# Two chained cross-attentions: stores of weighted values and loads of x moved on the DMA queue of the first half

## The chip, the cores and the metric

The kernel runs on one core of a Trainium2 chip. The core has a matrix engine (TensorE, PE in the profile), a vector engine (VectorE, DVE), a scalar engine (ScalarE, ACT), a general engine (GpSimd, POOL) and SyncE (SP), which here does nothing but issue DMAs. Every engine works through its own list of instructions in order and waits on semaphores for the others. The metric is the device time of one execution in microseconds (us). A profiled execution gives the trace from which single durations are read.

## The reference

Two cross-attention layers over the same 128 context tokens for each of two batches, 2048 tokens of 512 features each, all in float32:

```python
# layer 0: 16 heads of 64
qh = (x @ Wq + bq);  kh = (ctx @ Wk + bk);  vh = (ctx @ Wv + bv)
attn = einsum('bqhd,bkhd->hbqk', qh, kh) * mask
attn = exp(attn - max(attn)) * mask           # one maximum over everything
attn = attn / (sum(attn, -1) + 1e-15)
x = layernorm(einsum('hbqk,bkhd->bqhd', attn, vh) @ Wo + bo + x) * gamma + beta
# layer 1: 16 heads of 32, ordinary softmax, no mask
x = layernorm(softmax(q @ k.T / sqrt(32)) @ v @ Wo.T + bo + x) * gamma1 + beta1
```

The maximum of layer 0 is over all heads, batches and tokens, so no block of it can be finished before all scores of layer 0 exist.

## The kernel before

The 4096 tokens are cut into 8 tiles of 512 (`t`), taken in 4 pairs (`p`); the 16 heads into 4 groups of 4 (`g`). A *block* is one tile and one group: four heads, 128 keys, 512 tokens each.

The *first half* of the program computes layer 0 up to the weighted values. It is a loop of 16 steps `i` (`p = i // 4`, `g = i % 4`); each step takes both tiles of a pair for one group, so two blocks, called A (tile 2p) and B (tile 2p+1) below. The order is written out by hand, each engine keeps it, and DMAs stand in SyncE's list where the program names them. A step runs:

- loads for later: in pairs 1 and 2 (steps 4 to 11) the x of the next pair, in 512 KB halves, one in the steps with g = 0 and g = 2, two in those with g = 1 (`load_x`, L236, issued by SyncE); masks by POOL's queue (L242).
- `queries_pair` (L355 on TensorE, 28 matmuls in seven products): the queries of both blocks, put together from shared products by additions on VectorE (L367, L369). Between them, `exponentials0` of the two blocks of the step before: VectorE takes the maxima that were loaded back (L438, L439), ScalarE exponentiates (L442), POOL multiplies by the mask (L443). A's comes behind the first product, B's near the end.
- `sums_of_folded` in some steps (L478): denominators of the step before the last, copied out of the accumulators by VectorE and ScalarE (L449) and stored (L450).
- `scores0` of A: eight matmuls (L404), then VectorE masks the scores and takes a maximum for each key and pair of heads (L417, tile `top`). The maxima have to be the same on all 128 partitions, so they go through DRAM: a store of 1 KB (L426, `top_dram`) and a load of all 256 numbers to every partition, 128 KB (L429, tile `every`). The load waits, on SyncE, until the store has landed.
- `attend0` of A of the step before: TensorE multiplies probabilities and values (L499; L492 for denominators where they aren't folded), ScalarE copies the result out (L503), SyncE stores it, 512 KB (L504, `u_dram`).
- `scores0` of B, then `attend0` of B of the step before, in the same way.

The last step's maxima (both blocks) stay on the chip (`last4`) and are neither stored nor loaded. `shift` (L464) and `fold` (L470) prepare the folded denominators. Tile `u` has three buffers, x has four buffers in each of two pools, which the pairs use in turn. `wkv1`, the weights of keys and values of layer 1 (2 MB), is loaded at step 4, L542 and L543, and the output weights of layer 0 (2 MB) at step 13, L515.

The *second half* then normalises the weighted values, projects them, and runs layer 1; its order is written out too, and it is not touched.

Of the kernel before, what the change touches and what calls it, by code (L numbers as in the profile page):

```python
# [24 lines left out]
def two_cross_attentions(  # L25
# [28 lines left out]
    nc = tc.nc  # L54
# [14 lines left out]
    def where(t):  # L69
        return t // SPB, (t % SPB) * TB  # L70
# [18 lines left out]
    def sc_tiles(name, shape):  # L89
        return [p_sc.tile([P, *shape], F32, tag=f"sc{n}", name=f"{name}_{n}") for n in range(2)]  # L90
# [4 lines left out]
    def av_tile(name):  # L95
        return p_av.tile([P, TB], F32, tag="av", name=name)
# [28 lines left out]
    def chunks(w):  # L125
        return w.rearrange("(c p) m -> p c m", p=P)
# [6 lines left out]
    def row(pool, v, name, tag=None):  # L133
# [5 lines left out]
    u_dram = {  # L139
        (t, g): dram.tile([P, 2 * TB], F32, tag=f"u_{t}_{g}", name=f"u_{t}_{g}")  # L140
        for t in range(NB)
        for g in range(NG)
    }
    top_dram = {
        (t, g): dram.tile([P, 2], F32, tag=f"top_{t}_{g}", name=f"top_{t}_{g}")
        for t in range(NB)
        for g in range(NG)
    }
# [67 lines left out]
    with tc.tile_pool(name="w1", bufs=1) as w1, tc.tile_pool(name="a2", bufs=2) as a2, tc.tile_pool(  # L216
# [13 lines left out]
        def load_x(t, halves=range(2)):  # L230

            b, q0 = where(t)
            pool, tag = (big, "big") if t // 2 % 2 else (xs, "xt")
            for h in halves:
                xt = pool.tile([P, 2, TB], F32, tag=tag, name=f"xt_{t}_{h}")
                nc.sync.dma_start(xt, xT[b, q0 // TB, h])  # L236
                xts.setdefault(t, []).append(xt)

        def load_mask(t):
            b, q0 = where(t)  # L240
            m = a4.tile([P, TB], F32, tag="mask", name=f"mask_{t}")
            nc.gpsimd.dma_start(m, maskT[b, :, q0 : q0 + TB])  # L242
            return m
# [145 lines left out]
            add(c12, product(3, s4[:, g], b22, mm_tile), c12)  # L389

        tops0, probs0, pairs0 = {}, {}, {}
        FOLDED = [n for n in range(NB // 2 * NG - 2) if n % NG != NG - 2]
        last4 = w1.tile([P, 4], F32, tag="last4", name="last4")
        order = [(2 * p + n, g) for p in range(NB // 2) for g in range(NG) for n in range(2)]

        def scores0(t, g):

            b, _ = where(t)
            st = sc_tiles(f"st_{t}_{g}", [2, TB])
            for n in range(2):  # L400
                q = queries.pop((t, 2 * g + n))
                for j in range(2):
                    rows = slice(j * DK, (j + 1) * DK)
                    nc.tensor.matmul(  # L404
                        st[n][:, j, :], k0[rows, 2 * g + n, b * K : (b + 1) * K], q[rows, :],
                        start=True, stop=True,
                    )
            pair = fours.tile([P, 2, 2, TB], F32, tag="p1", name=f"sm_{t}_{g}")
            n0 = 2 * (order.index((t, g)) - len(order) + 2)
            if n0 >= 0:  # L410
                top = last4[:, n0 : n0 + 2]
            else:
                top = a2.tile([P, 2], F32, tag="top", name=f"top_{t}_{g}")
            pairs0[t, g] = pair
            for n in range(2):
                sm = pair[:, n]
                nc.vector.tensor_tensor_reduce(  # L417
                    out=sm, in0=st[n], in1=masks[t].unsqueeze(1).to_broadcast([P, 2, TB]),
                    scale=1.0, scalar=-3.4028234e38, op0=ALU.mult, op1=ALU.max,
                    accum_out=top[:, n : n + 1],  # L420
                )
                probs0[t, 2 * g + n] = sm
            if n0 >= 0:
                return

            nc.sync.dma_start(top_dram[t, g], top)  # L426
            every = a2.tile([P, 2 * P], F32, tag="every", name=f"every_{t}_{g}")
            flat = top_dram[t, g].rearrange("p n -> (p n)").unsqueeze(0)
            nc.sync.dma_start(every, flat.to_broadcast([P, 2 * P]))  # L429
            tops0[t, g] = every  # L430
# [16 lines left out]
        def store_sums(t, g, ps, copy=nc.scalar.copy):  # L447
            den = a2.tile([P, TB], F32, tag="den", name=f"dens0_{t}_{g}")
            copy(den, ps)  # L449
            nc.sync.dma_start(  # L450
                den_rows(den_dram, t, g), den.rearrange("(j n) q -> j n q", n=32)[:, 0, :]
            )
# [32 lines left out]
        def attend0(t, g):  # L485

            b, _ = where(t)
            p = [probs0[t, 2 * g + j // 2][:, j % 2, :] for j in range(4)]
            if order.index((t, g)) // 2 not in FOLDED:
                ps = av_tile(f"den0_{t}_{g}")  # L490
                for j in range(4):
                    nc.tensor.matmul(ps[32 * j : 32 * (j + 1), :], ones, p[j], start=True, stop=True)  # L492
                store_sums(t, g, ps)
            u = a3.tile([P, 2, TB], F32, tag="u", name=f"u0_{t}_{g}")
            for half in range(2):
                ps = av_tile(f"psu0_{t}_{g}_{half}")
                for j in range(4):
                    d = (4 * g + j) * DK + half * 32
                    nc.tensor.matmul(  # L499
                        ps[32 * j : 32 * (j + 1), :], v0[:, b, d : d + 32], p[j],  # L500
                        start=True, stop=True,
                    )
                nc.scalar.copy(u[:, half, :], ps)  # L503
            nc.sync.dma_start(u_dram[t, g], u.rearrange("p j q -> p (j q)"))  # L504

        bo0s, g0s = row(const, bo0, "bo0"), row(const, g0, "g0")
        b0cs = columns(const, b0c, "b0c")
# [12 lines left out]
        for i in range(len(order) // 2):  # L520
            p, g = i // NG, i % NG
            steps0 = order[2 * i : 2 * i + 2]
            if p == 0 and g == 2:
                for t in (2, 3):
                    load_x(t)
                    masks[t] = load_mask(t)
            elif 0 < p < NB // 2 - 1:
                for n in ((0,), (1, 2), (3,), ())[g]:
                    load_x(2 * p + 2 + n // 2, (n % 2,))
                if g > 1:  # L530
                    t = 2 * p + g
                    masks[t] = load_mask(t)
            if p == 0:
                for e in (2 * g, 2 * g + 1):
                    keys0(e)
            if i == 1:
                for n in range(E // TB):
                    values0(1, n)
            if i == 4:
                w = w1.tile([P, 2 * ND, TB], F32, tag="first", name="wkv1")  # L540
                wk1s, wv1s = w[:, :ND, :], w[:, ND:, :]
                nc.sync.dma_start(wk1s, chunks(wk1))  # L542
                nc.sync.dma_start(wv1s, chunks(wv1))  # L543
            if i == 12:
                sums0(0, w1, "sums0", 1)
            if i == 13:
                load_wo0()

            if i == 0:
                queries0(0, 0)  # L550
                queries0(0, 1)
            else:
                queries_pair(p, g, order[2 * i - 2 : 2 * i])
                if i - 2 in FOLDED:
                    sums_of_folded(i - 2)
            if i == len(order) // 2 - 1:
                for n in range(NG):
                    fetch_u(0, n)
            scores0(*steps0[0])
            if i == 0:  # L560
                queries0(1, 0)
                queries0(1, 1)
                weight_sums(1)
            else:
                if i - 1 in FOLDED:
                    shift(i - 1, 0)
                    fold(i - 1, 0)
                attend0(*order[2 * i - 2])
                if i - 1 in FOLDED:
                    shift(i - 1, 1)  # L570
            if i == 0:
                token_sums_1(0)
            elif g == NG - 1 and p + 1 < NB // 2:
                token_sums_1(p + 1)
            scores0(*steps0[1])
            if i == 0:
                for n in range(E // TB):
                    values0(0, n)
                token_sums_2(0)
                weight_sums(2)  # L580
            elif i < len(order) // 2 - 1:
                attend0(*order[2 * i - 1])
                if i - 1 in FOLDED:
                    fold(i - 1, 1)
            if g == NG - 1 and p + 1 < NB // 2:
                token_sums_2(p + 1)
            if i in (1, 2):
                weight_sums((3, 0)[i - 1])
# [45 lines left out]
        for n in range(2):  # L634
            t, g = order[n - 2]
# [439 lines left out]
    def store(t, i):  # L1075
        b, q0 = where(t)
        nc.sync.dma_start(out[b, q0 + i * P : q0 + (i + 1) * P, :], ys.pop((t, i))[0])
# [91 lines left out]
    t = NB - 1  # L1169
# [78 lines left out]
```

## Time and profile before

| | us |
|---|---|
| time before, median of 3 runs | 953.12 |
| lowest, highest | 951.63, 958.23 |
| profiled execution | 951.15 |
| its span, first to last instruction | 949.4 |

One profiled execution was read, with a mean granted TensorE clock of 0.995 of full speed. Of the DMA queues, SyncE's (q1) moved 155.64 MB in 65536 packets, with 49.2% of the time of the 16 DMA engines. Of the span's 30-us stretches between 40 and 370 us, TensorE is busy all 30 us in four, and for at least 28.2 us in every one. The first half's steps lie between some 30 and 370 us.

How to read it: times of instructions are from the start of the span. A timeline line has start, duration, engine, source line, operation, output and input tiles, count, and in brackets the idle time of that engine before it and what ended it. In a list of waits a line has who waited for whom, then the total in us, how often, and the longest. SPq is SyncE's issuing side: a line there is the issue of a DMA, not its transfer. Matmuls are pipelined and their ends are modelled, so a distance between starts says more of TensorE than its busy share.

### The profile page before, as it was taken

How to read it: one execution, taken by the hardware profiler on the slowest of the kernel's cores; microseconds unless marked ns; L12 is line 12 of the kernel's file. 1: busy time of each engine (PE TensorE's matmuls, PEld its weight loads, DVE VectorE, ACT ScalarE, POOL GpSimd, SP SyncE). 2: the span in 40 equal slices, each digit the busy share in tenths (PEclk: the TensorE clock that was granted, in tenths of full speed). 3: DMA queues.
4: the chain of work that ended last, by engine and by line, in shares of the span. 5: the costliest groups of instructions: out<-in, count | busy, mean ns of one | idle time of the engine just before them, and what ended most of it. 6: DMA issues, size and time to landing. Idle time of an engine off the chain costs nothing.

```text
span 949.4 us, 12453 instructions
## 1 busy us (share of the span) xinstructions
PE 924.2 (97%) x4404; PEld 444.0 (47%) x4404; DVE 695.3 (73%) x1026; ACT 378.2 (40%) x837; POOL 491.3 (52%) x403
## 2 busy tenths in 40 slices
PE   8999999999999999999999999999999999999996
PEld 4444333333333334356474564654744645546532
DVE  1577777877887885044929959969779699599777
ACT  1055445445645554213535333325234153154051
POOL 1043335534543335864682683764854936735343
PEclk9999999999999999999999999999999999999998
DMA  9414253323322525662987757656758567444401
GB/s 337 139 51 144 58 167 112 117 79 96 95 68 63 153 76 206 179 193 67 305 278 234 298 165 261 250 183 235 253 167 295 165 229 305 137 161 155 133 35 56
DMA packets 67326, 159.07 MB, mean 168 GB/s; under 512 B 10496, under 2 KB 14336, under 8 KB 63680
## 3 DMA queue, kind: packets, MB, share of 16 engines
q1 hardware_dynamic: 65536, 155.64, 49.2%
q0 software_dynamic: 1152, 2.10, 0.8%
q8 instruction: 35, 0.57, 0.3%
q10 hardware_dynamic: 576, 0.53, 0.2%
q14 instruction: 27, 0.22, 0.1%
HBM read 101.46 MB, written 56.78 MB: 167 GB/s over the span
## 4 chain that ended last, share of the span: by engine, by line
PE 45%; DVE 12%; DMA 2%; issue 2%; POOL 2%; ACT 1%; SPq 0%; POOLq 0%; DVEq 0%; ACTq 0%
PE pso L690 17%; PE pso L1039 8%; PE psq L829 6%; PE mx L881 3%; PE u L1009 3%; PE psq L867 2%; DVE e L922 2%; PE ps L355 1%; DVE sums L917 1%; DVE bn L672 1%; DVE y L1046 1%; DVE top L894 1%; PE psu L499 1%; DVE top L903 1%; PE psk L605 1%
## 5 line engine op out<-in xcount | busy, mean ns | idle before, releaser
L443 POOL TENSOR_TENSOR sm<-sm,mask 128x1024 f32<-128x1024 f32 x64 | 150.3, 2368 | 207.9 <-ACT sm L442 171.6
L690 PE MATMUL pso<-wo,uT 128*128 128x512 f32 x512 | 227.3, 597 | 0.3 <-POOL uT L192 0.3
L690 PEld LDWEIGHTS pso<-wo,uT 128*128 128x128 f32 x512 | 95.3, 190 | 120.5 <-issue 112.4
L898 ACT ACTIVATE e<-mx,less 128x128 f32<-128x128 f32 x224 | 78.7, 376 | 121.4 <-DVE less L895 116.3
L442 ACT ACTIVATE sm<-sm,ncs 128x1024 f32<-128x1024 f32 x64 | 70.0, 1141 | 113.1 <-DVE ncs L439 113.1
L1039 PE MATMUL pso<-wq,ctx 128*128 128x512 f32 x256 | 114.1, 597 | 0.0
L677 POOL TENSOR_TENSOR rstd<-rstd,mhalf 128x1 f32<-128x1 f32 x64 | 37.5, 585 | 135.6 <-DVE shift L681 135.6
L417 DVE CUSTOM_DVE_ANT_1 sm<-st,mask 128x1024 f32<-128x1024 f32 x64 | 75.6, 1216 | 19.0 <-DMA mask<-in_maskT_dram 12.1
L192 POOL TENSOR_TENSOR uT<-uT,r 128x1024 f32<-128x1024 f32 x32 | 79.4, 2496 | 18.2 <-DMA uT<-u 10.1
L355 PE MATMUL ps<-xt,wq 128*128 128x512 f32 x180 | 83.4, 599 | 0.0
L697 DVE TENSOR_TENSOR z<-pso,z 128x512 f32<-128x512 f32 x32 | 21.7, 679 | 78.8 <-PE pso L690 57.1
L367 DVE TENSOR_TENSOR q<-ps,q 128x512 f32<-128x512 f32 x75 | 51.8, 691 | 36.3 <-PE ps L355 31.7
L1039 PEld LDWEIGHTS pso<-wq,ctx 128*128 128x128 f32 x256 | 47.3, 190 | 56.2 <-issue 51.3
L470 DVE TENSOR_TENSOR fold<-fold,sm 64x2048 f32<-64x2048 f32 x22 | 65.0, 2954 | 5.4 <-ACT fold L464 4.9
L499 PE MATMUL psu<-sm,v 128*32 128x512 f32 x512 | 62.2, 598 | 4.0 <-ACT dens L449 4.0
L1054 ACT ACTIVATE y<-y,shift,rstd 128x512 f32<-128x512 f32 x30 | 23.3, 809 | 107.5 <-POOL shift L682 107.5
L922 DVE STREAM_TRANSPOSE e<-e 128x2048 f32<-128x2048 f32 x28 | 64.7, 2312 | 1.0
L404 PE MATMUL st<-q,k 64*128 64x512 f32 x256 | 63.6, 615 | 0.0
L707 POOL TENSOR_TENSOR y<-z,g 128x512 f32<-128x512 f32 x32 | 40.9, 1278 | 42.4 <-ACT z L705 42.4
L355 PE MATMUL ps<-t,s 128*128 128x512 f32 x120 | 56.4, 592 | 0.0
L355 PEld LDWEIGHTS ps<-xt,wq 128*128 128x128 f32 x180 | 33.2, 190 | 46.5 <-issue 46.2
L705 ACT ACTIVATE z<-z,shift,rstd 128x512 f32<-128x512 f32 x32 | 26.4, 828 | 66.9 <-POOL shift L682 66.9
(157 smaller groups left out, 1506.7 us busy)
## 6 DMA issues: line engine op xcount, KB each, us to landing
e<-e SPq DMA_DIRECT2D x28, 1024.0 KB
p<-e SPq DMA_DIRECT2D x28, 1024.0 KB
u<-u SPq DMA_DIRECT2D x32, 512.0 KB
uT<-u SPq DMA_DIRECT2D x32, 512.0 KB
xt<-in_xT_dram SPq DMA_DIRECT2D x16, 512.0 KB
z<-in_x_dram SPq DMA_DIRECT2D x32, 256.0 KB
r<-r SPq DMA_DIRECT2D x32, 256.0 KB
out_dram<-y SPq DMA_DIRECT2D x32, 256.0 KB
```

What stands on the lines that cost most here:

```text
L192: nc.gpsimd.tensor_tensor(u, u, r.unsqueeze(1).to_broadcast([P, 2, TB]), ALU.mult)
L355: nc.tensor.matmul(ps, w[:, c, :], x[c] if isinstance(x, tuple) else x[:, c, :], start=(c == 0), stop=(c == 1),)
L404: nc.tensor.matmul(st[n][:, j, :], k0[rows, 2 * g + n, b * K : (b + 1) * K], q[rows, :], start=True, stop=True,)
L417: nc.vector.tensor_tensor_reduce(out=sm, in0=st[n], in1=masks[t].unsqueeze(1).to_broadcast([P, 2, TB]), scale=1.0, scalar=-3.4028234e38, o ...
L442: nc.scalar.activation(s, s, AF.Exp, bias=ncs[:, i + n : i + n + 1])
L443: nc.gpsimd.tensor_tensor(s, s, masks[t].unsqueeze(1).to_broadcast([P, 2, TB]), ALU.mult)
L470: nc.vector.tensor_tensor(f, f, p[half_keys(n)], ALU.add)
L499: nc.tensor.matmul(ps[32 * j : 32 * (j + 1), :], v0[:, b, d : d + 32], p[j], start=True, stop=True,)
L690: nc.tensor.matmul(ps, uTs[t, n // 2][:, n % 2, i * P : (i + 1) * P], wo0s[n // 2][:, n % 2, :], start=(n == 0), stop=(n == NE - 1),)
L898: nc.scalar.activation(e[:, :, r * NQ + i, :], ps[1][:, r - 2, i, :].rearrange("p (k q) -> p k q", q=32), AF.Exp, bias=less[:, r - 2, i : ...
L922: nc.vector.transpose(flat, flat)
L1039: nc.tensor.matmul(ps, ctxs[t][g][:, i * P : (i + 1) * P], wo1s[:, g, :], start=(g == 0), stop=(g == NG - 1),)
```

## The change

Both kinds of large DMA of a step are kept in a list of things to issue, `behind`, and issued at one place, in `scores0`: directly behind the store of maxima and ahead of the load that waits for it. So a store of weighted values goes out behind the next block's store of maxima (the blocks of the last step flush the list too, though they store no maxima). The stores of the last three blocks are issued at once, as before, and so are the loads of x of pair 1, at step 2. The loads of x for pairs 2 and 3 go behind A's store of maxima of the same step. Nothing else is changed.

```diff
         tops0, probs0, pairs0 = {}, {}, {}
+        behind = []
...
                 probs0[t, 2 * g + n] = sm
+            if n0 < 0:
+                nc.sync.dma_start(top_dram[t, g], top)
+            for transfer in behind:
+                transfer()
+            behind.clear()
             if n0 >= 0:
                 return
 
-            nc.sync.dma_start(top_dram[t, g], top)
             every = a2.tile([P, 2 * P], F32, tag="every", name=f"every_{t}_{g}")
...
-            nc.sync.dma_start(u_dram[t, g], u.rearrange("p j q -> p (j q)"))
+            store = lambda: nc.sync.dma_start(u_dram[t, g], u.rearrange("p j q -> p (j q)"))
+            behind.append(store) if order.index((t, g)) < len(order) - 3 else store()
...
                 for n in ((0,), (1, 2), (3,), ())[g]:
-                    load_x(2 * p + 2 + n // 2, (n % 2,))
+                    behind.append(lambda n=n, p=p: load_x(2 * p + 2 + n // 2, (n % 2,)))
```

## The prediction

> **What bounds the kernel now.** First the page's busy shares: TensorE carries the time, and I ask how much of the first half (about 0 to 370 us, the only part that the edit touches) it still loses.
>
> ```profile
> PE 924.2 (97%) x4404; PEld 444.0 (47%) x4404; DVE 695.3 (73%) x1026; ACT 378.2 (40%) x837; POOL 491.3 (52%) x403
> ```
>
> Second, the waits of the compute engines up to 470 us (waited for, us in total, times, longest). The load of maxima holds VectorE nine times for 8.3 us, and near it in kind stand waits of TensorE on ScalarE's copy of denominators:
>
> ```profile
> DVE whole L438 <- DMA every<-top: 8.3, 9, 2.3
> ...
> PEld psu L499 <- ACT dens L449: 7.8, 10, 0.8
> ...
> PE psu L499 <- ACT dens L449: 4.0, 5, 1.8
> ```
>
> Third, the timeline of the worst of these, which ties the two together. L438 waits 2.26 us for `every`; ScalarE's exponentials L442 start behind it; the copy L449 is queued behind those; and TensorE, having finished eight score products at 234.2 to 236.2, waits for that copy to free its accumulator before L499:
>
> ```profile
> 234.22 1.99 PE L404 MATMUL st<-q,k 64*128 64x512 f32 x8
> 234.55 0.42 DVE L438 TENSOR_REDUCE whole<-every 128x2 f32<-128x256 f32 x1 [2.26 <-DMA every<-top]
> ...
> 235.20 2.19 ACT L442 ACTIVATE sm<-sm,ncs 128x1024 f32<-128x1024 f32 x2 [6.54 <-DVE ncs L439]
> ...
> 237.30 0.56 ACT L449 COPY dens<-den 128x512 f32<-128x512 f32 x1
> ...
> 238.01 1.92 PE L499 MATMUL psu<-sm,v 128*32 128x512 f32 x16 [1.80 <-ACT dens L449]
> ```
>
> Fourth, SyncE's own waits and its timeline, for why `every` is late.
>
> ```profile
> SPq L429 <- DMA top<-top: 124.6, 29, 7.0
> ```
>
> ```profile
> 217.11 0.32 SPq L426 DMA_DIRECT2D top<-top  x1
> 220.35 0.32 SPq L429 DMA_DIRECT2D every<-top  x1
> 220.77 0.38 SPq L504 DMA_DIRECT2D u<-u  x1
> 223.48 0.32 SPq L426 DMA_DIRECT2D top<-top  x1
> 230.16 0.32 SPq L429 DMA_DIRECT2D every<-top  x1
> 230.57 0.38 SPq L504 DMA_DIRECT2D u<-u  x1
> 231.05 1.26 SPq L236 DMA_DIRECT2D xt<-in_xT_dram  x2
> ```
>
> Call the first tile's block of a step A, the second's B. A's store of maxima (217.11) has an empty queue and lands in 3.2 us; B's (223.48) goes out 2.7 us behind 512 KB of weighted values and needs 6.7. Over steps 1 to 14 of this timeline the median gap from L426 to L429 is 3.3 us for A (2.9 to 4.5) and 6.2 for B (4.1 to 7.4).
>
> **What the wait costs TensorE.** In an undisturbed step the first L404 and the first L499 after it lie 1.92 us apart (213.44 to 215.36). Six steps have more. Their B waits at L438 (near 148, 169, 235, 277, 320, 341 us) are 1.41, 0.75, 2.26, 0.85, 1.12 and 0.69 us; the distance there is 2.94, 2.33, 3.79, 2.44, 2.64 and 2.28, an excess of 1.02, 0.41, 1.87, 0.52, 0.72 and 0.36: each time the wait less some 0.36 us of slack. A seventh wait of B (0.27 us at 361.5) and two of A (0.43 and 0.47 at 140.8 and 268.8) cost TensorE nothing. The sum, 4.90 us, is nearly all that TensorE loses in the steps, since the 28 products between lie 12.2 us apart every time. It is the ceiling of any gain here.
>
> **The change, part by part.** *No compute instruction is added or removed;* the DMAs are the same in number and size. Two kinds move on SyncE's queue; the mask loads on POOL's queue and ScalarE's queue are not touched.
>
> *Stores of values.* 29 of 32 now follow the next store of maxima. B's store of maxima is then queued behind only A's `every`, 128 KB. It should land like an A store, in 3.3 us with 4.5 as the bad end, instead of 6.2: relief of 1.7 to 2.9 us. In the worst step it is 2.2 to 3.4, 2.8 in the middle (6.68 before), against 1.9 needed; in the one at 148 it is 2.4 to 3.6 (6.86 before) against 1.0. So all six stalls should go.
>
> *What takes the vacated place.* The store now lies between B's two transfers. SyncE issues it in 0.38 us inside the landing wait, so it costs nothing while the wait is over 0.4 us. Its transfer: in 201 to 204 us `every` and one store (655 KB together) go through in three slices, 1 us each, last column GB/s:
>
> ```profile
> 201.00:202.00 1.00, 1.00 (x6) 0.49 (x3) 1.00 (x4) 0.59 (x1) 0.00 (x0) 1.00 0.34 129
> 202.00:203.00 1.00, 1.00 (x3) 0.38 (x2) 1.00 (x2) 0.00 (x0) 0.00 (x0) 1.00 0.92 367
> 203.00:204.00 1.00, 1.00 (x4) 0.47 (x3) 1.00 (x3) 0.69 (x1) 0.00 (x0) 1.00 0.49 169
> ```
>
> At 350 GB/s 512 KB take 1.5 us, and data start some 1 to 2 us after issue, so the store is through about 2 to 4 us behind L426, when `every` is only being issued. Extra delay of `every`: 0 if hidden, 1.5 us if it queues whole. I take 0, because `every` itself needs 1 to 2.4 us from issue to its first data.
>
> The Trainium skill, "DMA: Bandwidth & Descriptors", section "Queues, rings and completion order", speaks against the change here: each DMA engine consumes a queue's descriptors in ring order, so a load issued behind 512 KB waits for them. By that rule with the whole 1.5 us charged, the relief at 235 us would be 2.8 less 1.5, a stall of 0.6 us would stay there, and the sum would be 4.3 instead of 4.9; no row of before shows a store directly ahead of this load, so the trace does not decide.
>
> *A's side.* A's `every` has a store of values ahead of it too now, and in steps 4 to 6 and 8 to 10 one or, at 152 and 239 us, two loads of x (up to 1.5 MB, 4.5 us). Issuing them costs 0.38 plus at most 1.26 us (the row of two above), inside 3.3. Data start 1.5 to 2.5 us behind L426 and are through at 4.5 to 5.5 with one load, 6 to 7 with two, while `every` would begin 4.3 to 5.7 behind it. Lateness by these bounds: 0 with a store alone, 0 to 1.2 with one load, 0.3 to 2.7 with two. A's L438 has room: at 203.65 its result is followed by L367 at 205.04, and TensorE needs that addition only for its sixth product group, some 8.6 us behind the step's start at 201.2. L438 may so run about 6.4 us behind the start before VectorE's seven additions (0.7 us each) reach B's turn late; it runs at 2.4 to 5.2 now, mostly 4.3 to 4.8, and `every` has some 1 us in hand. So up to about 2.5 us late (6.4 less 4.8, and the 1) cost nothing in a middling step. I book 0.3 us for the two double loads, with 0 and 2 as ends.
>
> *Cover for the rest.* A load of x goes out 8 to 9 us later (209.31 to behind 217.1); the last half of a pair, then near 175 us, is first read by VectorE at 195.3. A store of values goes 2 us (A) or 9 us (B) later; its buffer, one of three, is refilled three blocks of some 10.7 us after it was filled, so, with 9 us and a landing like the 6.7 above, some 16 us remain. If that cover were gone ScalarE's L503 would stop. The 2 MB of second-half weights (122.88) and the output weights (316.77) lose what stood ahead of them, go out about 1 us earlier and clear the queue sooner. The last store moved (359.0) goes behind the four fetches at 365.5 and is read only in the second half.
>
> *Sum.* 4.9 less 0.3 is 4.6 us, against the profiled execution's 951.15 (span 949.4 and 1.75 around it): 946.55. The median shown is 1.97 higher, so 948.5. TensorE is the bound on both sides of the handover, so I keep the gain whole. With no relief in half of the stalls it would be 950.7.
>
> **Rivals.** *Wait exchanged for wait:* the store's landing shrinks but `every` queues behind the moved 512 KB, and receipts are slow with a write behind them. For: B's stores need 3.8 us from their last data to the next issue with writes about, A's 2.2. Against: those stores had the write ahead, not behind. It gives 0 to 2 us, 951 to 953.5. *More than stated:* there is no more than 4.9 in the steps, and only noise takes it under 944.
>
> *Slower:* A's maxima become the bound. With values, x and a mask (POOL issues one near 241 us) in the queue, issue itself can block: the store at 242.03 took 2.20 us to issue, beside 0.38 elsewhere. If A's `every` came over 2.5 us late in a step, each further us would be paid by TensorE. Paid at 3 us late in all fourteen steps that would be 14 x 0.5 = 7, less 4.9: 955; at 4 us late 14 x 1.5 = 21, less 4.9: 969. It decides from 2.85 us late on average (4.9 / 14 = 0.35 above 2.5). Against it: only two steps carry that much.
>
> **How the numbers follow.** Forecast (946 to 950): 0.70. Exchange (950 to 953.5): 0.18. Slower than before: 0.09, of which 0.06 over 1% (9.5 us, about what a measurement tells from no change). Lower than 946: 0.03, of which 0.02 by over 1%. The range 945.5 to 953.0 holds the first two and leaves out the rest.
>
> **What would show it.** Right: L426 to L429 near 3.3 us for B as for A; the wait of L438 on `every` down from 8.3 to under 2 us; TensorE's wait on L449 gone; 1.92 us from L404 to L499 in every step; hence the same chain some 4.6 us earlier at 370 us. Wrong: waits of L438 moved to the steps at 152 and 239 us, products L355 no longer 12.2 us a step, a wait of L317 on x or of L503 on a store of values.

## The result, and the profile after

The changed kernel takes 955.01 us (median of 22 runs, 953.29 to 958.42) beside 953.25 us of 22 runs of the kernel before: ratio 1.003, 95% interval 1.0018 to 1.0042. It is some 3 us slower by the ratio (1.8 us by the two medians), where 4.6 us faster was forecast. The profiled execution took 954.71 us, span 952.9 us; compute work is unchanged, as the page's busy line shows against that of before.

```profile
PE 924.3 (97%) x4404; PEld 443.1 (46%) x4404; DVE 695.5 (73%) x1026; ACT 378.2 (40%) x837; POOL 491.9 (52%) x403
```

In the changed file the store of maxima is L425, their load L434, the read-back L443 (L438 before), the copy of denominators L454 (L449), the products with values L504 (L499), the store of values L509 (L504). The waits up to 470 us, as who waited for whom, total, times and longest:

```profile
DVE whole L443 <- DMA every<-top: 19.1, 15, 2.1
...
PEld psu L504 <- ACT dens L454: 7.8, 10, 0.8
...
PE psu L504 <- ACT dens L454: 6.8, 5, 1.7
```

VectorE's wait for the load of maxima has grown from 8.3 to 19.1 us and TensorE's behind it from 4.0 to 6.8. SyncE's wait for the landing of the store reads 104.2 us, after 124.6:

```profile
SPq L434 <- DMA top<-top: 104.2, 29, 7.2
```

That is not a store that lands so much sooner. The list counts from the end of SyncE's instruction before, and SyncE now issues the moved transfers within that time. From the issue of the store to that of the load, the 28 trips of steps 1 to 14 add up to 132.1 us before and 129.3 after: B's landing is quicker, 5.2 us in the mean after 6.0, and A's is slower, 4.0 after 3.4. SyncE's timeline of the stretch that was shown of before:

```profile
218.81 0.31 SPq L425 DMA_DIRECT2D top<-top  x1
219.21 0.38 SPq L509 DMA_DIRECT2D u<-u  x1
219.69 0.38 SPq L236 DMA_DIRECT2D xt<-in_xT_dram  x1
223.07 0.32 SPq L434 DMA_DIRECT2D every<-top  x1
225.17 0.32 SPq L425 DMA_DIRECT2D top<-top  x1
225.58 0.38 SPq L509 DMA_DIRECT2D u<-u  x1
230.63 0.32 SPq L434 DMA_DIRECT2D every<-top  x1
```

A's landing (L425 to L434) went from 3.2 to 4.3 us, B's from 6.7 to 5.5. B's gain is spent at once: its load is read 5.2 us after issue (230.63 to 235.82), 4.4 before (230.16 to 234.55). The timeline there still has the chain of before, 0.4 us shorter:

```profile
235.82 0.42 DVE L443 TENSOR_REDUCE whole<-every 128x2 f32<-128x256 f32 x1 [1.84 <-DMA every<-top]
235.91 1.99 PE L405 MATMUL st<-q,k 64*128 64x512 f32 x8
...
238.57 0.56 ACT L454 COPY dens<-den 128x512 f32<-128x512 f32 x1
239.28 1.92 PE L504 MATMUL psu<-sm,v 128*32 128x512 f32 x16 [1.38 <-ACT dens L454]
```

The step with two loads of x is worse. A's load, issued at 244.47, is itself behind 1.5 MB and ahead of B's store: it lands 4.3 us behind the issue of B's store, whose first packet starts only after 2.5 us (0.8 with nothing ahead), and B's store needs 7.3 us to the issue of its load.

```profile
239.94 0.32 SPq L425 DMA_DIRECT2D top<-top  x1
240.31 0.42 SPq L509 DMA_DIRECT2D u<-u  x1
240.83 1.21 SPq L236 DMA_DIRECT2D xt<-in_xT_dram  x2
...
244.47 0.33 SPq L434 DMA_DIRECT2D every<-top  x1
246.91 0.33 SPq L425 DMA_DIRECT2D top<-top  x1
247.33 0.38 SPq L509 DMA_DIRECT2D u<-u  x1
...
254.22 0.32 SPq L434 DMA_DIRECT2D every<-top  x1
```

Both readings of maxima of that step then hold VectorE, 2.05 us for A and 2.11 for B:

```profile
251.25 0.42 DVE L443 TENSOR_REDUCE whole<-every 128x2 f32<-128x256 f32 x1 [2.05 <-DMA every<-top]
...
258.31 0.42 DVE L443 TENSOR_REDUCE whole<-every 128x2 f32<-128x256 f32 x1 [2.11 <-DMA every<-top]
```

**Where the 3 us are in this pair of traces.** By starts of TensorE's first product: step 15 begins 3.2 us later than before (353.15 against 349.96). Over their plain 1.92 us, the distances from the first L405 to the next product add up to 7.9 us up to there, against 4.9. The six largest are 0.62, 1.59, 0.81, 1.45, 1.73 and 1.74 us, and the second and fifth stand behind the two steps with two loads of x; the largest stands behind step 12, in which nothing but stores of values was moved. The first product of the projection (L690, now L696) comes 1.7 us later still, counted from step 15. The rest of the span is 1.5 us shorter, with one stretch of 3.4 us at half the granted clock (1.7 us) fewer than in the trace of before. 3.2 + 1.7 - 1.5 = 3.4, and the spans differ by 3.5.

### The profile page after: what moved, and what is told of

Read it like the earlier page. It is cut to its first block, busy times and chain, and to the rows that moved or that the text cites. A ratio compares the mean times of both kernels' runs of the same rounds, so it can differ in the third digit from the quotient of the medians.

```text
span 952.9 us, 12439 instructions
## 1 busy us (share of the span) xinstructions
PE 924.3 (97%) x4404; PEld 443.1 (46%) x4404; DVE 695.5 (73%) x1026; ACT 378.2 (40%) x837; POOL 491.9 (52%) x403
## 4 chain that ended last, share of the span: by engine, by line
PE 45%; DVE 9%; DMA 2%; issue 1%; POOL 1%; ACT 0%; POOLq 0%; DVEq 0%; SPq 0%; ACTq 0%
PE pso L696 18%; PE pso L1045 9%; PE psq L835 6%; PE mx L887 3%; PE u L1015 3%; PE psq L873 2%; DVE e L928 1%; DMA uT<-u 1%; DVE sums L923 1%; DVE top L900 1%; DVE bn L678 1%; DVE top L909 1%; PE tr L750 1%; DVE y L1052 1%; DVE e L911 1%
## 5 line engine op out<-in xcount | busy, mean ns | idle before, releaser
L696 PE MATMUL pso<-wo,uT 128*128 128x512 f32 x512 | 227.4, 597 | 0.3 <-POOL uT L192 0.3
L696 PEld LDWEIGHTS pso<-wo,uT 128*128 128x128 f32 x512 | 95.2, 190 | 120.7 <-issue 113.5
L504 PE MATMUL psu<-sm,v 128*32 128x512 f32 x512 | 63.0, 598 | 6.8 <-ACT dens L454 6.8
L405 PE MATMUL st<-q,k 64*128 64x512 f32 x256 | 63.6, 615 | 0.0
```

The lines of the kernel that those rows point to most:

```text
L405: nc.tensor.matmul(st[n][:, j, :], k0[rows, 2 * g + n, b * K : (b + 1) * K], q[rows, :], start=True, stop=True,)
L504: nc.tensor.matmul(ps[32 * j : 32 * (j + 1), :], v0[:, b, d : d + 32], p[j], start=True, stop=True,)
L696: nc.tensor.matmul(ps, uTs[t, n // 2][:, n % 2, i * P : (i + 1) * P], wo0s[n // 2][:, n % 2, :], start=(n == 0), stop=(n == NE - 1),)
```

## The experiments

Each ran in five rounds beside the kernel before on the same chip. There are five sets of two to four kernels, and not all had the same chip, which matters: medians of before were 947.17 and 946.93 us in sets 1 and 2 (one chip), 950.05 and 949.99 in sets 3 and 4 (another), 951.05 in set 5 (a third). Which chip gave the result above is not known. Traces are of one execution each. For each run I give the *round trip* of the maxima: from the issue of their store to the last landing event of their load, as a mean over steps 1 to 14. The last column of the tables sums what TensorE's distances from scores to the next product have over 1.92 us in that trace. In the first two traces the round trip is 8.0 us (A) and 9.8 (B) before, 9.1 and 9.9 after.

**Set 1: the parts alone.** Values alone (the edit on the changed kernel):

```diff
-                    behind.append(lambda n=n, p=p: load_x(2 * p + 2 + n // 2, (n % 2,)))
+                    load_x(2 * p + 2 + n // 2, (n % 2,))
```

> The stores of weighted values stay behind the next store of maxima, the loads of x go back to the start of the step. Theory W (a 512 KB store directly behind the 1 KB store of maxima delays its landing, so that block A's load of maxima, on time before, comes late): block A still needs about 4.4 us from L425 to L434 in nearly every step (3.2 us before the change), block B still has some stores that need over 5 us, and the time is 953 to 955.5 us, not below before by more than 1 us. Rival X (the moved loads of x did the harm, the moved stores are good as predicted): block A is back at 3.0 to 3.5 us, TensorE's distances from L405 to L504 are 1.92 us in nearly all steps, and the time is 948 to 950 us.

x alone:

```diff
-            behind.append(store) if order.index((t, g)) < len(order) - 3 else store()
+            store()
```

> Only the loads of x are moved behind A's store of maxima; stores of values go out at once as before the change. Theory W (it is the write behind the store that delays the landing): with a read of 512 KB behind it A's store of maxima still lands in 3.0 to 3.5 us in the six steps with x, block B keeps its 6 us, and the time is 953 to 955 us, with some loss from A's load queueing behind 0.5 to 1 MB of x. Rival X: most of the loss of the change is here, 955 to 957 us. Rival Q (any 512 KB behind the store delays it, read or write alike): A's landing is 4.4 us in those six steps and 3.2 us in the others.

A's values alone, with x as before:

```diff
-            behind.append(store) if order.index((t, g)) < len(order) - 3 else store()
+            behind.append(store) if t % 2 == 0 and order.index((t, g)) < len(order) - 3 else store()
```

> Only the first tile's store of values is moved, behind B's store of maxima; the second tile's store goes out at once as before, so nothing stands directly behind A's store of maxima, and x as before. Theory W: A needs 3.0 to 3.5 us again, B about 3.2 to 4.6 us (nothing ahead, a write behind), the stalls of TensorE between L405 and L504 sum to under 1.5 us (4.9 before the change), time 948.5 to 950.5 us. Rival X: 948.5 us too, but then e1 is as fast as this one. Rival N (B's late maxima are not what holds TensorE): 953 us.

The same, with the list issued behind the load of maxima:

```diff
-            for transfer in behind:
-                transfer()
-            behind.clear()
...
             tops0[t, g] = every
+            for transfer in behind:
+                transfer()
+            behind.clear()
```

> As the run with the first tile's store alone, but that store is issued behind B's load of maxima, not between its store and its load. Theory W: neither store of maxima has a write before or directly behind it, both land in 3.0 to 3.5 us, L438's wait for the load is under 1 us in total, TensorE has 1.92 us from L405 to L504 in all steps: 948 to 949 us, as fast as or up to 1 us faster than the run before. Rival Q2 (the load itself needs the queue empty behind it): no better than it, 949 to 951 us. Rival N: 953 us.

| run | ratio | interval | round trip A, B | over 1.92 us in the steps |
|---|---|---|---|---|
| values alone | 1.0025 | 1.0011 to 1.004 | 7.8, 8.7 | 0 |
| x alone | 1.0021 | 1.0 to 1.0043 | 7.8, 9.0 | 1.3 |
| A's values alone | 0.9989 | 0.9971 to 1.0007 | 7.1, 8.2 | 0 |
| A's values behind the load | 0.9996 | 0.9979 to 1.0013 | 7.1, 7.0 | 0 |

The stalls of x alone stand in the two steps behind its double loads (B's store landed in 7.6 and 7.9 us there, 4 to 6.4 elsewhere). There is more of it than in the last column: in one of the two, TensorE's 28 products lay 12.79 us apart, not 12.21. So x does harm in the steps, as X has it, but its time is hardly clear of noise, and neither Q nor plain W fits: with reads alone behind it A's store landed in 3.4 to 3.8 us in the six steps with x, 2.7 to 3.2 in the others. With a write behind it, in values alone, it landed in 2.7 to 4.8. The last two runs cleared the steps as expected and yet gained next to nothing. So either N holds (B's late maxima are not what holds TensorE), or before had nothing to lose on this chip. And values alone was slower by 2 us without any stall in its trace.

**Set 2: before and after on that chip.** The kernel before, the changed kernel, the changed kernel with its last two moved stores put back (`len(order) - 3` made `- 5`), and A's values behind the load again.

> The kernel before once more, for its trace on the chip on which the next three run. If the landing of a store is as quick here as in the first experiments (a bare store of maxima 2.8 to 3.0 us), TensorE's stalls between scores and values sum to 0 to 2 us, not 4.9, so that there is little to gain; if it is as slow as in the trace before (3.2 us), 4 to 5.5 us. Ratio 1.000.

> The changed kernel once more, on the same chip. Theory of two causes: it loses 1 to 2 us at the end of the first half, whatever the chip (two stores of values stand ahead of the loads of residual rows, POOL waits for these rows at L201 and its mask products come late), and 0 to 4 us in the steps, mostly in the two steps with two loads of x; in total 2 to 4 us slower than before, ratio 1.002 to 1.004. Rival S (all loss is in the steps): the distance from the last step to the first L696 is that of before within 0.3 us.

> The changed kernel, but the stores of the last five blocks, not three, are issued at once, so that no store of values is moved behind the four fetches and ahead of the loads of residual rows. Theory of two causes: POOL's wait at L201 and the distance from the last step to the first L696 are back at those of before (within 0.3 us), the steps are those of the changed kernel, and it is 1 to 2 us faster than the changed kernel: ratio to before 1.000 to 1.002. Rival S: as slow as the changed kernel.

> The first tile's stores alone, behind B's load of maxima, once more beside before and after on one chip. Both theories: no stall in the steps, the end of the first half as before. It should beat before by what before loses in its steps on this chip (0 to 2 us if stores land quickly, 4 to 5.5 us if they don't) and the changed kernel by 2 to 6 us.

Before again (0.9998) lost 0.57 us in its steps, not 4.9: in this trace its B round trip is 8.7 us, and nearly all of the gain forecast is not there to be had. After again: 1.0015 (0.9997 to 1.0033), round trips 8.4 and 8.9, losses in the steps behind the two double loads alone. The tail put back: 1.0018 (1.0 to 1.0035), as slow as the change, which speaks for S. A's values behind the load: 0.9989 (0.9968 to 1.0011).

**Set 3: second tile's values, the place, the tail.** B's values alone (`t % 2 == 1`, last five blocks at once), everything behind the load (the list moved as in the diff above, on the changed kernel), the last two moved stores alone, and values without these two (`- 5`).

> Only the second tile's stores of values are moved, behind the next step's first store of maxima (those of the last two steps go out at once; x as before). Theory W: A's store of maxima with a 512 KB write behind it lands in 3.7 to 4.4 us in most steps, B's still needs 4 to 6 us with a store ahead of it, and the time is 1 to 3 us over before, ratio 1.001 to 1.003. Theory X (x is what costs in the steps, A has room for a late landing): A lands late all the same but TensorE's stalls stay under 1 us, ratio 0.999 to 1.001.

> Everything that the change moves is moved, but behind the load of maxima instead of between the store and the load. Theory P (the place between store and load is what harms): A's store lands in 2.8 to 3.2 us in all steps and its load comes at once; in the steps with two loads of x B's store of maxima still queues behind them and lands in 5 to 7 us, so that a stall of up to 1 us may stay in the two steps after; ratio 0.999 to 1.001, 1 to 2 us faster than the changed kernel. Rival (x harms wherever it stands behind A's store): TensorE still loses about 2 us in the two steps, ratio 1.002.

> Only the two last moved stores of values (second tile of step 13, first tile of step 14) are moved as in the change; all else as before. Theory T (they delay the loads of residual rows, on which POOL waits ahead of the last mask products): L201 starts 1 to 2.3 us later behind the end of the steps, the first L696 comes 21 to 22 us behind the transpose L632 (20.4 to 20.7 otherwise), and the time is 0.5 to 1.5 us over before, ratio 1.0005 to 1.0015. Rival: POOL has room, 20.4 to 20.7 us, ratio 1.000.

> Stores of values of both tiles behind the next store of maxima, x as before, and the stores of the last five blocks at once. Theory T: the first run with the values alone lost 2 us or so over its trace by its last two stores; without them 20.4 to 20.7 us from the transpose to the first L696, no stall over 0.5 us in the steps, ratio 0.998 to 1.000. Rival Z (stores of values in that place cost something that the steps do not show): 1.002 to 1.003 as in that run.

| run | ratio | interval | round trip A, B | over 1.92 us in the steps |
|---|---|---|---|---|
| B's values alone | 1.0122 | 1.0093 to 1.015 | 8.6, 10.2 | 8.8 |
| everything behind the load | 1.0059 | 1.0037 to 1.0082 | 7.8, 9.5 | 5.9 |
| last two stores alone | 1.0013 | 0.9993 to 1.0033 | 7.6, 9.6 | 3.7 |
| values without these two | 1.0006 | 0.9986 to 1.0027 | 8.4, 9.4 | 1.9 |

B's values alone was worse than any theory had it. Its store goes from a place where the queue was idle, 8 us ahead of A's maxima, into A's round trip; A's load comes later, B's store queues behind it and behind A's values, which go out at once as before. With A's values out of the way too (the last line of the table, on the same chip) the loss is gone within the noise. TensorE's longest wait in the steps of any run stands here:

```profile
149.54 1.99 PE L405 MATMUL st<-q,k 64*128 64x512 f32 x8
153.89 3.30 PE L504 MATMUL psu<-sm,v 128*32 128x512 f32 x16 [2.37 <-ACT dens L454]
```

and that wait costs a second time. In windows of 2 us of this run (start and end, length, busy time of each engine, then the granted clock, DMA share and GB/s) TensorE's granted clock falls behind it (and once more behind a wait of 2.08 us at 242.5):

```profile
150.00:152.00 2.00, 1.52 (x8) 0.39 (x4) 1.53 (x4) 0.91 (x1) 0.00 (x0) 1.00 0.84 340
152.00:154.00 2.00, 0.11 (x4) 0.14 (x8) 2.00 (x4) 1.98 (x4) 1.63 (x1) 1.00 0.09 33
154.00:156.00 2.00, 2.00 (x12) 0.59 (x15) 0.82 (x3) 2.00 (x2) 2.00 (x2) 0.58 0.14 37
156.00:158.00 2.00, 2.00 (x12) 0.57 (x6) 2.00 (x1) 0.90 (x3) 1.60 (x2) 0.57 0.58 229
```

Everything behind the load overturns P: A's store was clean (2.8 to 3.3 us in all but the last two steps), but B's then landed in 5.0 to 7.1 us in all but two, since what is issued behind A's load stands ahead of B's store. It is the worst of the versions that move both tiles' values. The last two stores alone settled nothing within its interval, nor did the values without these two: its trace has stalls of 0.65 and 0.87 us and 21.4 us from the transpose to the first L696, contrary to T, and its interval holds both T's ratios and part of Z's.

**Set 4: doses.** The changed kernel without its double loads and without the tail (`load() if g == 1 else behind.append(load)`, and `- 5`); the double loads alone; all four halves of x at once, in the step with g = 1; and POOL's L201 placed behind the mask products.

```diff
-                for n in ((0,), (1, 2), (3,), ())[g]:
+                for n in ((), (0, 1, 2, 3), (), ())[g]:
```

```diff
         attend0(*order[-3])
-        residual(0, 0)
...
         exponentials0(*order[-2])
+        residual(0, 0)
```

> The changed kernel with two parts taken back: the two loads of x in the steps with g = 1 go out at the start of the step as before, and the stores of the last five blocks at once. Theory D (the loss in the steps is that of the two double loads: A's load late behind them, B's store of maxima late behind that): no landing of B over 6.5 us, TensorE's stalls in the two steps that follow fall under 0.5 us each, ratio 0.998 to 1.001. Rival E (every transfer between store and load costs its share): 1.001 to 1.003, stalls spread over the steps.

> The kernel before with just the two double loads of x moved behind A's store of maxima. Theory D: A's read-back of maxima and B's store both late in two steps only, B's landing there 7 to 8.5 us, stalls of 0.6 to 1.8 us in each of the two steps that follow (also between products), ratio 1.001 to 1.003, like all of x moved (1.0021). Rival E: half of that or less, 1.000 to 1.001.

> As all of x moved, but all four halves of a pair's x (2 MB) in the step with g = 1, behind A's store of maxima. Theory D, dose doubled: 1 MB more ahead of A's load is 3 us more, not hidden any longer, so the two steps that follow lose 3 to 5 us each; if TensorE's gaps get over some 2.1 us its granted clock halves for 3.4 us as well (1.7 us more each). Ratio 1.006 to 1.014. Rival E (a fixed price for each transfer, wherever it stands): as all of x moved, 1.002.

> The changed kernel, but POOL's first addition of a residual row (L201) is placed behind the mask products of the last step's first block instead of ahead of them, so that these no longer wait for the load of the row. Theory T (tail): the first of these mask products starts 4 to 5.5 us behind the transpose L632 (8.03 in the first trace of the changed kernel, 6.35 in the second) and the first L696 comes 20.3 to 20.7 us behind it (21.96, 20.49), so 0 to 1.7 us faster than the changed kernel, ratio 1.000 to 1.003. Rival: mask products earlier but the first L696 as late as before, since r and u come by other DMAs of the same queue.

The double loads alone: 1.0049 (1.0022 to 1.0075), more than D had for all of x; four at once: 1.0065 (1.0039 to 1.009), in D's range and over E's 1.002, which came from another chip. With four, SyncE waits 10.4 us for B's store:

```profile
240.44 0.32 SPq L425 DMA_DIRECT2D top<-top  x1
240.85 1.82 SPq L236 DMA_DIRECT2D xt<-in_xT_dram  x4
244.00 0.33 SPq L434 DMA_DIRECT2D every<-top  x1
244.42 0.62 SPq L509 DMA_DIRECT2D u<-u  x1
246.82 0.32 SPq L425 DMA_DIRECT2D top<-top  x1
257.23 0.32 SPq L434 DMA_DIRECT2D every<-top  x1
```

and A's load is now so late that the query products too, which do not wait in the kernel before, wait for VectorE's additions:

```profile
PE psu L504 <- ACT dens L454: 3.5, 5, 1.6
PE ps L355 <- DVE q L367: 2.5, 2, 1.8
PE ps L355 <- DVE q L369: 1.4, 2, 0.7
```

By the traces a larger dose costs more: in the two steps behind the double loads TensorE loses 2.4 and 2.7 us with two loads, 3.6 and 3.9 with four. The times do not tell the doses apart. And without the double loads the change is still slow, 1.0036 (1.0013 to 1.0058), no faster than with them on this chip (1.0023, the run with L201 moved): D is not the whole of it, and the prices of the parts do not add up to that of the change. Its trace has no stall behind the two double steps and 1.33, 1.55, 0.88, 0.24 and 0.81 us behind steps 4, 6, 8, 10 and 12, four of which load one x. Round trips there are 8.6 and 9.4. E had the spread right; the ratio lies over its 1.001 to 1.003, its interval does not.

With L201 out of the way: 1.0023 (1.0004 to 1.0041), mask products 3.8 us behind the transpose, first L696 20.8. That is earlier than T had the one and later than it had the other.

**Set 5: before's gain, and the change again.** A's values behind the load, and the changed kernel, on a third chip.

> First tile's stores alone, behind B's load of maxima. B from the issue of its store of maxima to the landing of its load in 7 us or so (8.6 to 10 before the change), A in 7, no stall of TensorE over 0.2 us in the steps. If the kernel before loses 3.5 to 5 us in its steps on this chip: ratio 0.995 to 0.997. If only about 1 us: 0.998 to 1.000.

> The changed kernel on the same chip. Sum of store and load of maxima for B within 0.5 us of the kernel before (a quicker store, a slower load), for A some 1 us longer than before, stalls in the steps after the two double loads of x; ratio 1.001 to 1.004, and 3 to 8 us slower than the run beside it.

The first: 0.9963 (0.9942 to 0.9983), 947.18 us against 951.05, faster than both kernels. Round trips are 7.3 and 7.5 us, with none of TensorE's distances over 1.92. SyncE's timeline shows the order (the store is L512 here), and the waits up to 470 us what is left:

```profile
215.46 0.32 SPq L425 DMA_DIRECT2D top<-top  x1
218.63 0.32 SPq L434 DMA_DIRECT2D every<-top  x1
221.83 0.32 SPq L425 DMA_DIRECT2D top<-top  x1
224.85 0.32 SPq L434 DMA_DIRECT2D every<-top  x1
225.26 0.86 SPq L512 DMA_DIRECT2D u<-u  x2
226.21 1.93 SPq L236 DMA_DIRECT2D xt<-in_xT_dram  x2
```

```profile
DVE whole L446 <- DMA every<-top: 1.8, 3, 0.8
```

Both round trips run with no 512 KB transfer ahead of them or within them, and all large transfers share the 10 us between B's load and the next step's A. The store landed in 2.6 to 3.6 us, but in 4.0 to 4.9 in steps 9 and 10. The changed kernel beside it: 1.0023 (1.0003 to 1.0044), round trips 8.9 and 9.5, 6.3 us slower than that run by the medians (953.44 less 947.18).

## Why the prediction was wrong, point by point

The mechanism of the loss was right, and the step that failed is its cure: B's maxima were to come 1.7 to 2.9 us sooner with nothing to pay on B's load and 0.3 us on A's side. In the first two traces B's store gained 0.8 us, B's load lost 0.9, and A's round trip became 1.1 us longer.

*What bounds the steps: right.* B's late maxima hold TensorE by way of L438, L442 and L449, and taking that away is worth about what was worked out where the kernel loses it: 3.9 us by the medians of set 5, against 4.9 summed from the trace of before. But this ceiling is not the same everywhere: the trace of before in set 2 has 0.57 us, and the version that gains in set 5 gained nothing clear of noise in sets 1 and 2.

*"Relief of 1.7 to 2.9 us", with "extra delay of `every`: 0": wrong, and the step that failed first.* Store and load were costed apart, and A's load, ahead of B's store, was taken to be on time. In the first two traces the store's mean for B fell from 6.0 to 5.2 us, the load's rose from 3.8 to 4.7: the round trip is 9.9 us after 9.8. The rival "wait exchanged for wait", given 0.18, is what B did. B's store did land in 3.0 to 3.3 us, as forecast, in four steps (1, 7, 11 and 13): in these A's load had landed by 1.6 us behind the issue of B's store. In nine of the other ten it landed 2.3 to 4.4 us behind, and B's store took 4.6 to 8.1. The bound of 1.5 us that the text kept for a queued load was nearer to the 0.9 measured than 0. The rule of ring order of the Trainium skill ("DMA: Bandwidth & Descriptors", section "Queues, rings and completion order") agrees with the runs of set 1: with A's values behind the load B's load takes 3.9 us, with them between store and load 4.9. Yet the whole 1.5 us, charged to B's load alone, leaves the sum at 4.3, as the prediction has it; what that leaves out is A's side.

*A's side, "0 with a store alone": wrong.* A's store landed 0.6 us later in the mean and its load came 0.5 us later, so A's round trip grew from 8.0 to 9.1 us. The rival named a reason, slow receipts with a write behind them, and the runs bear it out in part: with values alone (set 1) A's store stayed under 3.0 us in nine of fourteen steps, with the same write behind it. What else it takes is open. (Its 3.8 us from B's last data to the next issue is 3.2 in the median of the 14 steps by the starts of the packets; the 2.2 for A is right.) The room of A's read-back was judged rightly: A's own lateness showed between query products only with two or more loads of x. But the step missed that B's store stands in the same queue 5.5 to 7 us behind A's, so that A's lateness is handed to B, which has no room. B's values alone shows this: they move into A's trip and nowhere else, B's round trip grows to 10.2 us (9.6 with the last two stores alone, on the same chip), and the ratio is 1.0122.

*The double loads, "0.3 us, with 0 and 2 as ends": mis-sized.* 3.3 us of stalls stand behind these steps in the first trace of the change, and alone they cost 0.49% (0.22 to 0.75), 4.7 us, on the chip of set 4.

*Cover for the rest.* Neither L317 waited for x nor L503 for a store of values, as said; the weights of the second half did not go out earlier (123.12 after 122.88). That the last moved stores cost nothing does not fit the first trace of the change. One of them more stands ahead of the loads of residual rows there, and POOL, which has L201 ahead of the mask products, waited longer. Waits in before and after, from about 370 us on:

```profile
POOL z L201 <- DMA z<-in_x_dram: 9.0, 1, 9.0
```

```profile
POOL z L201 <- DMA z<-in_x_dram: 11.1, 1, 11.1
```

In the six executions where the first mask product starts over 7 us behind the transpose, the first L696 follows it by 13.9 us each time, 21.0 to 22.5 us behind the transpose; where it starts earlier other DMAs hold L696, mostly at 20.4 to 20.8. So late residual rows cost up to some 2 us in some executions, but that the moved stores are the cause is not shown: alone they gave 1.0013 (0.9993 to 1.0033), and in set 2 the distance is 21.3 us in before and 20.5 in the change.

*Left open:* that the change gains nothing is explained by the two round trips; that it is 3 us slower is so only in part. Values alone in set 1 was 2 us slower than before with clean steps; its trace explains 1 us by the tail. Without the double loads (set 4) the change was 3.4 us slower, of which the trace of one execution shows no more than half, and of the 11.6 us of B's values alone the stalls and the two drops of the clock, less the 3.7 us of before, give 8.5. No trace of before was taken on the chips of sets 3 to 5, so how much before loses there is inferred from the run nearest to it (3.7 us with the last two stores alone). No run has A's values between store and load on the chip of set 5, so whether the gain there needs the place behind the load is not shown.

## What to carry to other kernels

A round trip through DRAM (small store, wait, load) is one item on its queue: the time to shorten is from the issue of the store to the landing of the load, and a transfer put into the wait between them is paid by the load (3.9 to 4.9 us here) and, where the next round trip follows closely, by that. Look for the stretch in which the queue has no such trip open and put the large transfers there; here that was behind the second of two trips, not between or within them. Before counting on a gain from a wait of 1 or 2 us, look at how much of it is there in another execution and on another chip.

## What the runs showed of the hardware

In steps 1 to 14 of all twenty traces, take the stores of 1 KB whose last 8-byte packet started by 1.1 us after issue, so that nothing held them up ahead. From issue to the issue of their load, 155 of them with nothing behind on SyncE's queue took 2.6 to 3.5 us but for nine (up to 4.9; seven of these have a load of masks of POOL's queue in that time); the median is 3.0. With a 512 KB write directly behind, 129 took 2.7 to 5.0, in the median 3.4 and in 46 cases over 4. With only loads of x behind, ten took 3.4 to 3.8. In the trace after, ten of A's stores took over 4 us; in nine of these, 11 to 14 of the 16 landing events had come by 3.0 us: the delay is in the last few.

TensorE's waits of 2.08 and 2.37 us (B's values alone) and one of 2.00 (the double loads alone) were each followed within 0.8 us by 3.4 us at half the granted clock, 1.7 us more. Another of 2.00 us (everything behind the load, at 173.8) was not, nor were those of 1.80 and 1.68 in the steps of the first two traces. In the second half a wait of 1.89 us was followed by it in the trace before (at 809.6) and not in the trace after (814.6), and in values alone two gaps of 0.68 and 1.13 us, close together, were (469.2). So no one length of gap decides here. The Trainium skill, "TensorE: Matmul & The Clock Gate", section "Why this matters for your kernels", advises against idle gaps over about 3 us between bursts; in this case gaps of 1.9 to 2.4 us were enough in some executions, and the measurement decides.
